# Fetching gates and head outputs earlier in the output projection of a mixture-of-experts attention kernel

## The chip, the cores and the metric

The kernel runs on one core of one Trainium2 chip. The metric is the time of one execution on the device in microseconds (us). All times of the profile come from one profiled execution. Five engines are spoken of: TensorE (PE, with weight loads as PEld), VectorE (DVE), ScalarE (ACT), GpSimd (POOL) and SyncE (SP). SP does nothing here but issue DMAs, one after the other, and wait before an issue when the data or the buffer is not ready.

## The reference

N = 1250 rows of 1024 numbers pass through a graph layer, and then through one transformer layer whose attention has 16 heads of 64, with 8 experts for each head's values and outputs, of which a gate picks two per row. Cut to what matters here:

```
gv, go = gate(x, Wsel_v), gate(x, Wsel_o)          # per row, head, expert: 0 but for the two picked
v   = einsum('bsd,bhse,hedp->bhsp', x, gv, Wv)     # values: gated sum over 8 experts
att = softmax(q k^T / 8)
o   = einsum('bhst,bhtp->bhsp', att, v)
src2 = einsum('bhsp,bhse,hepd->bsd', o, go, Wo)    # outputs: gated sum over heads and experts
```

A residual, a norm, a feed-forward layer with its norm, and a last residual follow. Everything is float32; the kernel splits each operand of a matmul into a high and a low part and adds three products (`dot`, L154 to L156).

## The kernel before, in words

The program is in stages: the graph layer, the gates with the queries and keys, then a long stretch in which values, attention and outputs are interleaved by hand, and the feed-forward layer. The long stretch and most of the outputs lie in `manual_schedule`, where each engine takes its instructions in the order in which the code issues them. Three generators are woven together; each `yield` hands over to the next one.

- `values` makes a head's values in 40 pieces, four for each of ten row tiles (the tenth has 98 rows, the others 128). After a tile's last piece DVE multiplies the product by the gates into `ve` (L897); after every second tile it adds the eight experts in halves, 4, 2 and 1 (L903, L906), and splits the sum into two parts (L908, L909). For the pair with the 98-row tile it does this twice, once for each tile. The weights of the next head are loaded to `w_raw`, rounded on ACT (`w_hi`, L138) and subtracted on DVE (`w_lo`, L144); the fourth block is done in the first pieces of the next head.
- `attention` takes 80 chunks of 256 queries, five for each head, in eight steps each: scores on PE (L721), the maximum on DVE (`most`, L724), the exponential on ACT (`p`, L725), sixteen copies `turned<-p` (L736, eight issued by SP and eight by POOL), a transposition on DVE (L798), a split of the result on ACT and DVE (`att_hi`, L755; `att_lo`, L760), and the products with the values (`po`, L778, evacuated at L785). A chunk's work spreads over the steps of the chunks that follow it.
- `outputs` starts with a preamble of 16 steps beside the last 16 pieces of `values`, and then takes 80 steps m: 16 blocks (eight pairs of heads, four experts at a time) times five chunks of 250 rows. A step multiplies two row tiles, each in two halves; each half is 24 matmuls and one add into the accumulator (L1006), and each step of the main loop holds eight yields.

The pieces of `values` end with head 15; the attention chunks that are left (75 to 79, and two more rounds for what trails) then alternate with the steps of `outputs`, about one step for each chunk. These are the steps from about 1860 to 2010 us.

In `outputs`, `load` issues on SP the gates of a chunk (`gb`, two DMAs of 250 KB, two buffers), the heads' outputs (`oc`, two of 125 KB, one buffer) and the inverse sums (`r`, two of 62.5 KB, one buffer). `gated` (L946 to L948) adds, scales and multiplies them on DVE, in place in `gb`; `parts_of` splits it on ACT and DVE (`go_hi`, L955; `go_lo`, L957). `acc_load` brings a row tile of the running sum (`z_d`, 500 KB by two DMAs at L150). Accumulators 1 to 8 lie in the memory of `zT`, which the last pieces of `values` still read, so the profile names them `zT` and the last one `gate_v`. In step m the order was:

```
            if following:
                found = load(*order[following[0]], following[1])
...
                    nc.vector.tensor_tensor(acc[t][:, cols], acc[t][:, cols], p, ALU.add)
                    if following and half:
                        parts[i] = parts_of(found, i)
                    elif following and i == 0:
                        found = gated(*found)
                    elif raw is not None:
                        after.append(rounded(raw))
```

so that gates, `oc` and `r` of chunk m+1 were all issued at the start of step m, and used by `gated` after the first of the step's four halves. `w_raw` has two buffers.

Of the kernel before, what the change touches and what calls it, by code (L numbers as in the profile page):

```python
# [11 lines left out]
F32 = mybir.dt.float32  # L12
# [5 lines left out]
ALU = mybir.AluOpType  # L18
# [8 lines left out]
HD = 64  # L27
NX = 8
# [4 lines left out]
P = 128  # L33
NT = 10
# [10 lines left out]
QB = 250  # L45
# [27 lines left out]
def gnn_ffn_kernel(  # L73
# [23 lines left out]
    nc = tc.nc  # L97
# [591 lines left out]
    v_of = {}  # L689
# [164 lines left out]
    def values(att_pool, pool, now):  # L854

        todo = {}

        def later(k, what, *args):
            todo.setdefault(k, []).append((what, args))

        piece = 0
        for h in range(H):
            raw, new = {}, [None] * 4

            def load(h, k, raw=raw):
                raw[k] = loaded(wv[h, k])

            def first_part(k, raw=raw, new=new):
                new[k] = high(raw[k])

            def second_part(k, raw=raw, new=new):
                new[k] = rounded(raw.pop(k), None, new[k])

            if h + 1 < H:

                for at_, k in ((22, 0), (36, 1), (37, 2), (39, 3)):
                    later(piece + at_, first_part, k)
                for at_, k in ((23, 0), (37, 1), (38, 2), (40, 3)):
                    later(piece + at_, second_part, k)
                for at_, k in ((16, 0), (22, 1), (28, 2), (37, 3)):  # L880
                    later(piece + at_, load, h + 1, k)
            v_of[h] = att_pool.tile([P, NT, P], F32R, name="v2", bufs=2)

            ts = range(NT) if h < H - 1 else [*range(NZ, NT), *range(NZ)]
            for t in ts:
                n = min(P, N - P * t)
                p = bank([n, 512])
                for d in range(ND):
                    dot(p, z_of(t, d), [part_[:, 512 * (d % 2) : 512 * (d % 2 + 1)] for part_ in now[d // 2]],
                        d == 0, d == ND - 1)  # L890
                    if d % 2 == 0:
                        continue
                    if d == ND - 1:
                        gate = gate_v[:n, t, NX * h : NX * (h + 1)]
                        if t % 2 == 0:
                            ve = pool.tile([P, 2, NX, HD], F32, name="ve", bufs=1)
                        nc.vector.tensor_tensor(ve[:n, t % 2], p.rearrange("p (e k) -> p e k", e=NX),  # L897
                                                gate[:, :, None].to_broadcast([n, NX, HD]), ALU.mult)
                    if d == ND - 1 and t % 2:
                        for n, k in ((P, slice(0, 2)),) if n == P else ((P, slice(0, 1)), (n, slice(1, 2))):  # L900
                            x = ve[:n, k]
                            for half in (4, 2):
                                nc.vector.tensor_tensor(x[:, :, :half], x[:, :, :half], x[:, :, half : 2 * half],  # L903
                                                        ALU.add)
                            v = pool.tile([P, 2, HD], F32, name="v")[:n, k]
                            nc.vector.tensor_tensor(v, x[:, :, 0], x[:, :, 1], ALU.add)  # L906
                            v2 = v_of[h][:n, t - 1 + k.start : t - 1 + k.stop, :]
                            nc.vector.tensor_copy(v2[:, :, :HD], v)  # L908
                            nc.vector.tensor_tensor(v2[:, :, HD:], v, v2[:, :, :HD].bitcast(F32), ALU.subtract)  # L909
                    yield  # L910
                    for what, args in todo.pop(piece, ()):
                        what(*args)
                    piece += 1
            now = new
# [4 lines left out]
    def outputs(acc_pool, pool):  # L919

        last = QW * (NC - 1)

        def load(j, half_e, c):

            cols = slice(QB * c, QB * (c + 1))
            gb = pool.tile([P, 4, QB], F32, name="gb", bufs=2)
            for h2 in range(2):
                row = NX * (2 * j + h2) + 4 * half_e
                g = g_d[row : row + 4, cols]
                nc.sync.dma_start(gb[HD * h2 : HD * (h2 + 1)],  # L930
                                  bass.AP(tensor=g.tensor, offset=g.offset, ap=[[0, HD], [N, 4], [1, QB]]))
            o = pool.tile([P, 2, QB], F32, name="oc")
            for h2 in range(2):
                nc.sync.dma_start(o[HD * h2 : HD * (h2 + 1)], o_d[j][h2][:, cols].rearrange("(m f) n -> f m n", m=2))
            r = pool.tile([P, QB], F32, name="r")
            for h2 in range(2):
                for a, b in ((QB * c, min(QB * (c + 1), last)), (max(QB * c, last), QB * (c + 1))):
                    if b > a:
                        at_ = a + (NC * QW - N if a >= last else 0)
                        nc.sync.dma_start(r[HD * h2 : HD * (h2 + 1), a - QB * c : b - QB * c],  # L940
                                          r_d[j][h2 : h2 + 1, at_ : at_ + b - a].to_broadcast([HD, b - a]))
            return gb, o, r

        def gated(gb, o, r):

            nc.vector.tensor_tensor(o[:, 0], o[:, 0], o[:, 1], ALU.add)  # L946
            nc.vector.tensor_tensor(o[:, 0], o[:, 0], r, ALU.mult)
            nc.vector.tensor_tensor(gb, gb, o[:, 0:1].to_broadcast([P, 4, QB]), ALU.mult)  # L948
            return gb

        def parts_of(gb, i):

            mine = slice(KT * i, KT * (i + 1))
            hi = pool.tile([P, 4, KT], F32R, name="go_hi", bufs=2)
            nc.scalar.copy(hi, gb[:, :, mine])  # L955
            lo = pool.tile([P, 4, KT], F32R, name="go_lo", bufs=2)
            nc.vector.tensor_tensor(lo, gb[:, :, mine], hi.bitcast(F32), ALU.subtract)  # L957
            return hi, lo

        order = [(j, half_e) for j in range(NP) for half_e in range(2)]  # L960
        blocks = {k: [wo[j, 4 * half_e + i] for i in range(4)] for k, (j, half_e) in enumerate(order)}
        steps = [(k, c) for k in range(len(order)) for c in range(NQ)]

        def acc_load(t):
            acc.append(acc_pool(t))
            move(acc[t], z_d[t])


        w, raw = [], []
        for i in range(4):  # L970
            raw.append(loaded(blocks[0][i]))
            yield
            if i % 2:
                yield
                for _ in range(2):
                    w.append(rounded(raw.pop(0)))
                    yield
        found = load(*order[0], 0)
        acc_load(0)
        yield  # L980
        yield
        found = gated(*found)
        yield
        parts = []
        for i in range(2):
            parts.append(parts_of(found, i))
            yield
        after = []
        yield
        for m, (k, c) in enumerate(steps):  # L990
            raw = loaded(blocks[k + 1][c]) if c < 4 and k + 1 < len(order) else None
            following = steps[m + 1] if m + 1 < len(steps) else None
            if following:
                found = load(*order[following[0]], following[1])
            for i in range(2):
                t = 2 * c + i
                if k == 0 and t + 1 < NT:
                    acc_load(t + 1)
                for half in range(2):
                    cols = slice(512 * half, 512 * half + 512)  # L1000
                    p = bank([KT, 512])
                    for e in range(4):
                        dot(p, [part[:, e, :] for part in parts[i]], [part[:, cols] for part in w[e]], e == 0, e == 3)
                        if e == 1:
                            yield
                    nc.vector.tensor_tensor(acc[t][:, cols], acc[t][:, cols], p, ALU.add)  # L1006
                    if following and half:
                        parts[i] = parts_of(found, i)
                    elif following and i == 0:
                        found = gated(*found)  # L1010
                    elif raw is not None:
                        after.append(rounded(raw))
                    yield
            if c == NQ - 1:
                w, after = after, []
# [180 lines left out]
```

## Time and profile before

| what | value |
|---|---|
| median of 3 runs | 3000.13 us (2994.33 to 3004.78) |
| the profiled execution | 2998.75 us |
| its span | 2997.0 us |
| PE busy | 2858.0 us, 95% |
| PEld, DVE | 2357.3 us (79%), 2131.5 us (71%) |
| ACT, POOL | 993.4 us (33%), 568.9 us (19%) |
| granted TensorE clock, mean | 0.981 |
| DMA, mean | 129 GB/s |

The page cuts the span into 40 slices of 75 us; a digit is the busy share in tenths, and PEclk the clock granted to TensorE, also in tenths. In rows of instructions "L946" is line 946 of the kernel, "x2" a count; what stands in brackets is how long the engine stood idle before the row, and what ended that wait. Rows of the windows give the stretch, its length, the busy time of PE, PEld, DVE, ACT and POOL with the number of instructions, the granted clock, the DMA engines' busy share and GB/s.

### The profile page before, as it was taken

The numbers are of one execution on the slowest core, as the hardware profiler recorded it, in microseconds if no ns is written. First come the engines' busy times: TensorE is split into PE (matmuls) and PEld (weight loads), VectorE is DVE, ScalarE is ACT, GpSimd is POOL, SyncE is SP. The second block draws the span as 40 slices with busy tenths as digits, with TensorE's granted clock in tenths as the row PEclk, the third lists the DMA queues.
The fourth block names the chain that finished last, engine by engine and source line by source line (L and its number), as shares of the span: only waits on it lengthen the run. The fifth ranks groups of instructions, "written<-read, shape, count | busy, mean of one in ns | idle before, by whom it ended". The sixth has DMA issues, their size and how long they took to land. (4 is left out here: it accounts for less than half of the span.)

```text
span 2997.0 us, 40469 instructions
## 1 busy us (share of the span) xinstructions
PE 2858.0 (95%) x14018; PEld 2357.3 (79%) x14018; DVE 2131.5 (71%) x3668; ACT 993.4 (33%) x1706; POOL 568.9 (19%) x945
## 2 busy tenths in 40 slices
PE   6989899999999999999999999689999999999998
PEld 5767699978888887888888887567777777777787
DVE  7974488657877877887888778556666666666885
ACT  5772223324434433443434334221111111111222
POOL 2000011113333333333333333210000000000113
PEclk9999899999999999999999999889999999999999
DMA  3115465635555555555555455666444444444412
GB/s 116 56 43 155 145 174 161 194 83 147 139 137 143 136 135 126 136 135 149 138 141 150 129 145 132 156 166 162 114 120 122 116 118 123 113 119 122 108 47 91
DMA packets 229321, 385.46 MB, mean 129 GB/s; under 512 B 43369, under 2 KB 176489, under 8 KB 228946
## 3 DMA queue, kind: packets, MB, share of 16 engines
q1 hardware_dynamic: 176898, 273.49, 32.9%
q0 software_dynamic: 51888, 104.18, 14.5%
q10 hardware_dynamic: 320, 5.12, 0.5%
q8 instruction: 111, 1.82, 0.3%
q14 instruction: 104, 0.85, 0.1%
HBM read 220.73 MB, written 62.16 MB: 94 GB/s over the span
## 5 line engine op out<-in xcount | busy, mean ns | idle before, releaser
L155 PE MATMUL mm<-w_lo,zT 128*128 128x512 f32 (+1 forms) x1280 | 507.1, 396 | 13.1 <-DVE w_lo L144 13.1
L154 PE MATMUL mm<-w_hi,go_hi 128*125 128x512 f32 x1280 | 508.2, 397 | 2.1 <-ACT go_hi L955 1.2
L155 PE MATMUL mm<-w_lo,go_hi 128*125 128x512 f32 x1280 | 509.0, 398 | 0.0
L154 PE MATMUL mm<-w_hi,zT 128*128 128x512 f32 (+1 forms) x1280 | 507.4, 396 | 1.0 <-ACT w_hi L138 1.0
L156 PE MATMUL mm<-w_hi,go_lo 128*125 128x512 f32 x1280 | 506.6, 397 | 0.7 <-DVE go_lo L957 0.7
L156 PE MATMUL mm<-w_hi,zT 128*128 128x512 f32 (+1 forms) x1280 | 506.0, 395 | 0.0
L755 ACT CAST att_hi<-turned 128x512 fp32r<-128x512 f32 x400 | 239.5, 621 | 439.7 <-DVE turned L798 257.3
L736 POOL DMA_DIRECT2D turned<-p x640 | 342.5, 543 | 79.7 <-ACT p L725 44.3
L1006 DVE TENSOR_TENSOR zT<-zT,mm 125x512 f32<-125x512 f32 x256 | 175.1, 685 | 221.5 <-PE mm L156 217.5
L955 ACT CAST go_hi<-gb 128x500 fp32r<-128x500 f32 x160 | 98.3, 615 | 669.0 <-PE mm L155 280.5
L725 ACT ACTIVATE p<-side,most 128x1250 f32<-128x1250 f32 x160 | 209.0, 1306 | 330.4 <-DVE most L724 325.8
L724 DVE TENSOR_REDUCE most<-side 128x1 f32<-128x1250 f32 x160 | 230.9, 1443 | 113.1 <-PE side L721 111.9
L798 DVE STREAM_TRANSPOSE turned<-turned 128x1280 f32<-128x1280 f32 x160 | 232.4, 1490 | 111.0 <-DMA q<-kq_d 52.7
L154 PEld LDWEIGHTS mm<-w_hi,go_hi 128*125 128x125 f32 x1280 | 239.2, 187 | 63.2 <-ACT go_hi L955 1.5
L156 PEld LDWEIGHTS mm<-w_hi,go_lo 128*125 128x125 f32 x1280 | 238.8, 187 | 62.1 <-DVE go_lo L957 1.1
L155 PEld LDWEIGHTS mm<-w_lo,go_hi 128*125 128x125 f32 x1280 | 239.0, 187 | 59.3
L156 PEld LDWEIGHTS mm<-w_hi,zT 128*128 128x128 f32 (+1 forms) x1280 | 238.4, 186 | 59.7
L155 PEld LDWEIGHTS mm<-w_lo,zT 128*128 128x128 f32 (+1 forms) x1280 | 238.8, 187 | 53.2 <-DVE w_lo L144 18.2
L154 PEld LDWEIGHTS mm<-w_hi,zT 128*128 128x128 f32 (+1 forms) x1280 | 238.8, 187 | 36.0 <-ACT w_hi L138 1.2
L760 DVE TENSOR_TENSOR att_lo<-turned,att_hi 128x512 fp32r<-128x512 f32 x400 | 262.1, 681 | 0.0
L721 PE MATMUL side<-keys,q 128*128 128x512 f32 (+1 forms) x960 | 215.3, 360 | 30.5 <-ACT p L725 30.5
L721 PEld LDWEIGHTS side<-keys,q 128*128 128x128 f32 x960 | 182.9, 191 | 74.4 <-ACT p L725 32.7
(234 smaller groups left out, 4640.2 us busy)
## 6 DMA issues: line engine op xcount, KB each, us to landing
turned<-p SPq DMA_DIRECT2D x640, 80.0 KB
turned<-p POOLq DMA_DIRECT2D x640, 80.0 KB, 3.3
gb<-g_d SPq DMA_DIRECT2D x160, 250.0 KB
w_raw<-in_wv SPq DMA_DIRECT2D x64, 512.0 KB
w_raw<-in_wo SPq DMA_DIRECT2D x64, 512.0 KB
q<-kq_d POOLq DMA_DIRECT2D x80, 256.0 KB, 4.3
oc<-o_d SPq DMA_DIRECT2D x160, 125.0 KB
kq_d<-qk_hi SPq DMA_DIRECT2D x64, 156.2 KB
```

The lines of the kernel that those rows point to most:

```text
L154: nc.tensor.matmul(p, lhsT=lhs[0], rhs=rhs[0], start=start, stop=False)
L155: nc.tensor.matmul(p, lhsT=lhs[0], rhs=rhs[1], start=False, stop=False)
L156: nc.tensor.matmul(p, lhsT=lhs[1], rhs=rhs[0], start=False, stop=stop)
L721: nc.tensor.matmul(side[:, k0 : k0 + w], lhsT=q_of[n][:, part, P * i : P * (i + 1)], rhs=keys[:, k0 : k0 + w], start=(part == 0), stop=(pa ...
L724: nc.vector.tensor_reduce(most, side[:, :N], AX.X, ALU.max, negate=True)
L725: nc.scalar.activation(p[:, (2 * n + i) % 3, :N], side[:, :N], AF.Exp, bias=most, accum_out=inverse[h][:, 2 * c + i : 2 * c + i + 1])
L736: queue.dma_start(t[NB * a : NB * (a + 1), :, KA * b : KA * (b + 1)], both[NB * b : NB * (b + 1), :, KA * a : KA * (a + 1)])
L755: nc.scalar.copy(hi, x)
L760: nc.vector.tensor_tensor(lo, x, hi.bitcast(F32), ALU.subtract)
L798: nc.vector.transpose(turned[n][:, i], turned[n][:, i])
L955: nc.scalar.copy(hi, gb[:, :, mine])
L1006: nc.vector.tensor_tensor(acc[t][:, cols], acc[t][:, cols], p, ALU.add)
```

## The change

There are four edits.

1. `load` becomes `load_gates` and `load_o`, and step m fetches for chunk m+2. Its gates are issued at the start of step m; its `oc` and `r` right behind `gated` of chunk m+1.
2. Accumulators are loaded two row tiles ahead instead of one: 0 and 1 in the preamble, t+2 in the first five steps.
3. The preamble keeps its 16 steps and is written out by number. The first two weight blocks are rounded in the same steps as before (numbers 3 and 4); blocks 2 and 3 are loaded in those steps (before: 5 and 6), and rounded in 7 and 8 (before: 8 and 9). Chunk 0 is fetched in step 4, accumulator 0 in 5 (both before: 10), `gated` runs in 9 (before: 12), and chunk 1 is fetched there. Step 6 is the one in which the attention issues eight of its `turned` copies on SP.
4. In `values` one `ve` tile is made once, and the adds over the experts run over all 128 rows of both tiles of a pair, also for the pair with the 98-row tile. Rows 98 to 127 of that tile hold what an earlier tile left; the products read only the first 98.

```diff
-                        for n, k in ((P, slice(0, 2)),) if n == P else ((P, slice(0, 1)), (n, slice(1, 2))):
-                            x = ve[:n, k]
-                            for half in (4, 2):
-                                nc.vector.tensor_tensor(x[:, :, :half], x[:, :, :half], x[:, :, half : 2 * half],
-                                                        ALU.add)
...
+                        for half in (4, 2):
+                            nc.vector.tensor_tensor(ve[:, :, :half], ve[:, :, :half], ve[:, :, half : 2 * half],
+                                                    ALU.add)
+                        v = pool.tile([P, 2, HD], F32, name="v")
+                        nc.vector.tensor_tensor(v, ve[:, :, 0], ve[:, :, 1], ALU.add)
+                        v2 = v_of[h][:, t - 1 : t + 1, :]
...
+        def fetch(m, gates):
+            if m < len(steps):
+                (j, half_e), c = order[steps[m][0]], steps[m][1]
+                if gates:
+                    found.append(load_gates(j, half_e, c))
+                else:
+                    held[:] = load_o(j, c)
+
+        w, raw, found, held, parts = [], [], [], [], []
+        for begun in range(16):
+            if begun < 2:
+                raw.append(loaded(blocks[0][begun]))
+            if begun in (3, 4, 7, 8):
+                w.append(rounded(raw.pop(0)))
+            if begun in (3, 4):
+                raw.append(loaded(blocks[0][begun - 1]))
+            if begun == 4:
+                fetch(0, True)
+                fetch(0, False)
+            if begun == 5:
+                acc_load(0)
+            if begun == 9:
+                current = gated(found.pop(0), *held)
+                fetch(1, True)
+                fetch(1, False)
+            if begun in (11, 13):
+                parts.append(parts_of(current, len(parts)))
+            if begun == 14:
+                acc_load(1)
             yield
         after = []
-        yield
         for m, (k, c) in enumerate(steps):
             raw = loaded(blocks[k + 1][c]) if c < 4 and k + 1 < len(order) else None
-            following = steps[m + 1] if m + 1 < len(steps) else None
-            if following:
-                found = load(*order[following[0]], following[1])
+            following = m + 1 < len(steps)
+            fetch(m + 2, True)
             for i in range(2):
                 t = 2 * c + i
-                if k == 0 and t + 1 < NT:
-                    acc_load(t + 1)
+                if k == 0 and t + 2 < NT:
+                    acc_load(t + 2)
...
                     if following and half:
-                        parts[i] = parts_of(found, i)
+                        parts[i] = parts_of(current, i)
                     elif following and i == 0:
-                        found = gated(*found)
+                        current = gated(found.pop(0), *held)
+                        fetch(m + 2, False)
```

More of the change, by code (lines that the diff above doesn't have):

```diff
@@ L861, in values @@
         piece = 0
+        ve = pool.tile([P, 2, NX, HD], F32, name="ve", bufs=1)
         for h in range(H):
@@ L894, in values @@
                         gate = gate_v[:n, t, NX * h : NX * (h + 1)]
-                        if t % 2 == 0:
-                            ve = pool.tile([P, 2, NX, HD], F32, name="ve", bufs=1)
                         nc.vector.tensor_tensor(ve[:n, t % 2], p.rearrange("p (e k) -> p e k", e=NX),
@@ L899, in values @@
                     if d == ND - 1 and t % 2:
-                        for n, k in ((P, slice(0, 2)),) if n == P else ((P, slice(0, 1)), (n, slice(1, 2))):
-                            x = ve[:n, k]
-                            for half in (4, 2):
-                                nc.vector.tensor_tensor(x[:, :, :half], x[:, :, :half], x[:, :, half : 2 * half],
-                                                        ALU.add)
[L905 to L909, printed above, removed]
+                        for half in (4, 2):
[4 more added lines that the diff above has]
+                        v2 = v_of[h][:, t - 1 : t + 1, :]
+                        nc.vector.tensor_copy(v2[:, :, :HD], v)
+                        nc.vector.tensor_tensor(v2[:, :, HD:], v, v2[:, :, :HD].bitcast(F32), ALU.subtract)
                     yield
@@ L921, in outputs, with load_gates @@
         last = QW * (NC - 1)
-        def load(j, half_e, c):
+        def load_gates(j, half_e, c):
             cols = slice(QB * c, QB * (c + 1))
@@ L931, in load, with load_o @@
                                   bass.AP(tensor=g.tensor, offset=g.offset, ap=[[0, HD], [N, 4], [1, QB]]))
+            return gb
+        def load_o(j, c):
+            cols = slice(QB * c, QB * (c + 1))
             o = pool.tile([P, 2, QB], F32, name="oc")
@@ L941, in load @@
                                           r_d[j][h2 : h2 + 1, at_ : at_ + b - a].to_broadcast([HD, b - a]))
-            return gb, o, r
+            return o, r
         def gated(gb, o, r):
@@ L966, in acc_load @@
             move(acc[t], z_d[t])
-        w, raw = [], []
-        for i in range(4):
-            raw.append(loaded(blocks[0][i]))
-            yield
[L973 to L981, printed above, removed]
-        found = gated(*found)
[L983 to L986, printed above, removed]
+        def fetch(m, gates):
[26 more added lines that the diff above has]
+                acc_load(1)
             yield
         after = []
-        yield
         for m, (k, c) in enumerate(steps):
             raw = loaded(blocks[k + 1][c]) if c < 4 and k + 1 < len(order) else None
-            following = steps[m + 1] if m + 1 < len(steps) else None
-            if following:
-                found = load(*order[following[0]], following[1])
+            following = m + 1 < len(steps)
+            fetch(m + 2, True)
             for i in range(2):
                 t = 2 * c + i
-                if k == 0 and t + 1 < NT:
-                    acc_load(t + 1)
+                if k == 0 and t + 2 < NT:
+                    acc_load(t + 2)
                 for half in range(2):
@@ L1007, in outputs @@
                     if following and half:
-                        parts[i] = parts_of(found, i)
+                        parts[i] = parts_of(current, i)
                     elif following and i == 0:
-                        found = gated(*found)
+                        current = gated(found.pop(0), *held)
+                        fetch(m + 2, False)
                     elif raw is not None:
```

## The prediction

> **What bounds the kernel now.** I read the page first: how busy TensorE (PE) is, where it is not, and at what clock.
>
> ```profile
> PE 2858.0 (95%) x14018; PEld 2357.3 (79%) x14018; DVE 2131.5 (71%) x3668; ACT 993.4 (33%) x1706; POOL 568.9 (19%) x945
> ...
> PE   6989899999999999999999999689999999999998
> ...
> PEclk9999899999999999999999999889999999999999
> ```
>
> PE is the bound nearly everywhere; an edit beside a full PE is worth nothing. Slices 26 to 28 (from about 1870 us) are the hole in the stretch that the change touches: the "6" and "8", with a lowered clock. There the last attention chunks run beside the first output steps. Next, the stage windows, a steady attention chunk (15 us) against one turn-to-turn cycle of the hole:
>
> ```profile
> 1825.00:1840.00 15.00, 15.00 (x77) 12.67 (x77) 11.71 (x16) 5.95 (x10) 5.62 (x11) 1.00 0.48 109
> ...
> 1922.19:1949.93 27.74, 17.63 (x77) 14.42 (x76) 15.45 (x20) 7.81 (x14) 5.58 (x10) 0.76 0.60 150
> ```
>
> Both hold about 77 matmuls, yet the second takes 27.74 us. PE is busy for 17.63 of it (stretched by a granted clock of 0.76), VectorE (DVE) for 15.45, and the DMA engines for 0.60 x 27.74 = 16.6. No resource fills the cycle, so a chain of waits does. The waits of 1840 to 2060 us:
>
> ```profile
> ACT p L725 <- DVE most L724: 63.0, 11, 15.8
> ...
> DVE oc L946 <- DMA oc<-o_d: 38.8, 5, 10.3
> ...
> PE side L721 <- ACT p L725: 30.3, 4, 10.1
> ```
>
> PE waits for the exponentials, these for the row maximum on DVE, and DVE stands in `gated` before a load. Its timeline:
>
> ```profile
> 1901.18 0.69 DVE L1006 TENSOR_TENSOR acc<-acc,mm 125x512 f32<-125x512 f32 x1
> 1910.93 0.42 DVE L946 TENSOR_TENSOR oc<-oc 128x250 f32<-128x250 f32 x1 [9.06 <-DMA oc<-o_d]
> 1911.77 0.42 DVE L947 TENSOR_TENSOR oc<-oc,r 128x250 f32<-128x250 f32 x1 [0.43 <-DMA r<-r_d]
> ...
> 1913.34 1.45 DVE L724 TENSOR_REDUCE most<-side 128x1 f32<-128x1250 f32 x1
> ```
>
> And the sync queue (SP) shows why the load is late: it is issued behind eight transposing copies, a weight block and 500 KB of gates, right before its use.
>
> ```profile
> 1894.77 5.17 SPq L736 DMA_DIRECT2D turned<-p  x8
> 1899.99 0.60 SPq L127 DMA_DIRECT2D w_raw<-in_wo  x1
> 1900.63 1.87 SPq L930 DMA_DIRECT2D gb<-g_d  x2
> 1902.60 1.43 SPq L934 DMA_DIRECT2D oc<-o_d  x2
> 1904.08 1.25 SPq L940 DMA_DIRECT2D r<-r_d  x2
> 1905.43 4.39 SPq L150 DMA_DIRECT2D zT<-z_d  x4
> ```
>
> From issue (1902.60) to the end of the wait is 8.3 us. After about 2040 us the windows show PE at 60.00 of every 60 us until 2820, so nothing in those steps can win time.
>
> **Part 1, fetches ahead.** Today step m issues gates, `oc` and `r` for chunk m+1 at its start; `gated` uses them a quarter of a step later. After the change gates have a step and a quarter, and `oc` and `r`, issued behind `gated` of m+1, have a full step, 11.2 us even at PE's pace (48 matmuls by 0.233 from start to start) and more beside attention. With 8.3 us from issue to landing in the worst burst shown, the DVE wait goes. Only the order changes: per step the same 7 or 8 DMAs on SP, and none more on POOL.
>
> Its size, on the adds behind each step's first half (L1006): 1901.18, 1927.63, 1956.72, 1984.06, 2005.29, thus 26.5, 29.1, 27.3 and 21.2, together 104.1 us. In the cycles from one L946 to the next, 27.7, 27.5 and 26.2 us, the waits for `oc` and `r` are 10.8, 9.0 and 7.8; 16.9, 18.4 and 18.3 us remain. What comes next is no longer one wait: DVE needs 15.5 us busy, PE about 15.9 (48 x 0.233 for outputs, 12 score and 20 product matmuls at about 0.235 or 0.118 from start to start, 4.7), the DMA engines 16.6, SP's issues 14.7 (the six lines above). I take 18 us for each full cycle, which leaves DVE 2.5 us of its small waits (0.60 for `w_hi`, up to 1.9 for a matmul, both in the old cycles), and 15 for the last one, which has no new softmax. So 104.1 - (3 x 18 + 15) = **35 us**. Best case: cycles of 16.6 and 13.7, 40 us. Worst credible: 21 and 17, 24 us.
>
> The waits that this adds: gates of m+2 wait on SP for the buffer of chunk m, last read by `go_lo` at the end of step m-1; `oc`/`r` wait for `gated` on DVE, as each has one buffer. Behind them on SP stand the second accumulator load, the next weight block and the next eight `turned` copies, which in turn wait for the second softmax, later in DVE's order than `gated`: nothing that could start is held up. The price if it could: at most the interval from the start of a step to its first add, about 3 us per cycle, 12 in all. The accumulators a step earlier (1 MB per step either way) are hidden the same way: their first use is a step later; uncovered, each would cost its 2.2 us of issue, some 10 us in all.
>
> Two rules of the Trainium skill bear on this size. The granted clock fell to 0.76 in the cycle above and single matmuls went from 0.39 to 0.63 us. "TensorE: Matmul & The Clock Gate" (Part 1: The HAM clock gate) says that PE falls to half clock after about 3.4 us without work. With PE's gaps (8.8, 10.1, 8.4, 4.6 us) gone the clock returns, worth 17.63 - 15.9 = 1.7 us per cycle on PE; I add none, because DVE, not PE, sets 18, and it already covers it. Against the change stands "DMA: Bandwidth & Descriptors" (Issuing engines are not separate DMA queues): all queues end on the same 16 DMA engines, so a new order moves no byte faster. By its fabric ceiling of 435 GB/s the 4.17 MB of a cycle would take 9.6 us and never bind; by the trace they take 16.6. I use 16.6: a cycle cannot be much under it. That is why I stay above DVE's and PE's own sums, and why rival 1 is not small.
>
> **Part 2, first weights' loads.** Today load 3 stands on SP behind the `turned` copies (issued at 1875.38); ScalarE waits 5.63 us for it, DVE 6.32, and PE stands 3.0 us at 1885.36 and 4.0 at 1895.57. In the new order load 3 goes out when its buffer is free (`w_lo` of block 1, done at about 1868), and lands in some 4.1 us (load 0: 1858.99 to 1863.05), before it is wanted. Moved ahead of the same eight `turned` copies: load 3 (0.5 us of issue), two gates (1.3), two `oc` (1.4), two `r` (1.6), two accumulator copies (1.4), 6.2 us from 1867.5, so the copies start at about 1873.8, not 1870.17, and land near 1881. DVE's transposition of them, at 1887.06 today, comes due at about 1881 once its 6.3 us wait is gone. Net **6 us** (0 if the copies land 6 us later still; at most 10.8: those two PE gaps and 3.8 of slowed matmuls). The 3.1 us PE gap at 1870 stays: load 0 is where it was. Accumulator 1 is now asked for one piece before the last reader of its memory; SP holds for about 2 us, with the next weight block behind it, which is wanted ten us later: nothing.
>
> **Part 3, sums over all rows.** For the last pair of row tiles ten DVE instructions become five. Rows cost nothing: 98x512 and 128x512 both take 681 ns at L897. The ten take 904.23 to 907.15, 2.92 us; the five, as in other pairs (1897.90 to 1899.88), 1.98. So DVE is 0.94 us earlier once per head, right before each head switch:
>
> ```profile
> 904.23 0.74 DVE L903 TENSOR_TENSOR ve<-ve 128x256 f32<-128x256 f32 x2
> ...
> 907.15 0.69 DVE L760 TENSOR_TENSOR att_lo<-turned,att_hi 128x512 fp32r<-128x512 f32 x1
> 907.76 1.22 DVE L144 TENSOR_TENSOR w_lo<-w_raw,w_hi 128x1024 fp32r<-128x1024 f32 x1
> ...
> 909.03 0.50 PE L155 MATMUL mm<-w_lo,zT 128*128 128x512 f32 x1 [0.85 <-DVE w_lo L144]
> ```
>
> PE waits for exactly this `w_lo` at 14 switches, 0.73 to 0.85 us each. `w_lo` also needs `w_hi` from ScalarE (ready at 906.33 here, so it can start at 906.82). Switch by switch, the earlier of the two limits gives the whole wait in ten, 0.35 to 0.7 in three and nothing in one (at 1644.90), 9.7 us in all. I take **9**, between 3 (if ScalarE's load is late more often) and 9.7.
>
> **Sum.** 35 + 6 + 9, and 1 for two PE gaps of 0.9 and 0.7 us at 2019 and 2040 behind the same loads: 51 us. The profiled execution took 2998.75 us (span 2997.0), 1.4 under the median of 3000.13; so 2948 for such an execution, 2949 as a median. The end of the program is left as it is, give or take 3 us.
>
> **Rivals.** (1) The DMA engines bind: 16.6 us of work in an 18 us cycle, in bursts. For: single 10 us windows at a share of 1.06, and DVE's small waits for `turned` copies even in steady chunks. Against: the bursts now get the idle parts of the cycle. Cycles of 21, 24 us saved, 3 in part 2, 8 in part 3: 2965.
> (2) It doesn't do what it says: the wait for `oc` moves to `turned` or to the accumulators, cycles stay at 27, only part 3 remains: 2991. Against: the DMA engines are idle for 40% of each cycle.
> (3) Slower: in the 75 steps after 2040 us, today PE-bound, `oc`'s single buffer lets its load start only after `gated`. Of 11.2 us some 3 go to `gated` and issuing, 8 remain. If landing takes x us more than that, each step loses x; slower than before by over 0.3% from x = (51 + 9) / 75 = 0.8 us; at x = 1.1, 3031. For: 8.3 us were seen. Against: that was in a burst at a share near 1; in those steps the share is 0.44.
>
> **How the numbers follow.** Main case 0.58 (2936 to 2958), rival 1 0.24 (2957 to 2982), rival 2 0.07, rival 3 0.11. 0.3%, 9 us, is about what a measurement of this kernel can tell from no change. Faster 0.83 (main, rival 1 and a little of 2), same 0.06, slower 0.11. The range 2935 to 2984 leaves out rivals 2 and 3 and a thin tail. Its low end is the sum of best cases: 40 + 10.8 + 9.7 + 1.6 + 3 = 65.
>
> **What would show it.** Right: L946's wait for `oc` gone, cycles at 17 to 19 us, clock near 1.0 from 1890 on, PE's waits for `w_lo` L144 down from 13.1 us to about 4. Wrong: `turned` (L798) waiting for DMA several us per cycle (rival 1), or L946 waiting after 2040 us with PE under 60 of 60 (rival 3).

## The result, and the profile after

The median went from 2998.39 us (4 runs) to 2963.11 us (4 runs; 2959.1 to 2975.35), ratio 0.9887 with a 95% interval of 0.9853 to 0.9922. A second set, on another occasion, gave 2960.35 against 3000.68 us, 0.9875 (0.9858 to 0.9893). The profiled execution took 2961.16 us, span 2959.4, against 2998.75 and 2997.0 before.

So 38 us of the 51 forecast came by the profiled executions (35 by these medians, 40 by those of the second set). To see where, I cut both traces at the same instructions: the exponential (L725) of the first chunk, that of chunk 75, the add behind step 0's first half, that of step 4, and the end.

| stretch (us) | before | after | saved | forecast |
|---|---|---|---|---|
| start to first exponential | 633.7 | 633.7 | 0.0 | 0 |
| chunks 0 to 74 beside `values` (the head stage) | 1224.1 | 1222.3 | 1.8 | 9 (part 3) |
| chunk 75 to the add of step 0 (preamble) | 43.3 | 41.0 | 2.3 | 6 (part 2) |
| adds of steps 0 to 4 | 104.1 | 69.3 | 34.8 | 35 (part 1) |
| from there to the end | 991.7 | 993.0 | -1.3 | 1 |

From the page of the changed kernel, the slices of TensorE (PE) and its clock:

```profile
PE   6989899999999999999999999899999999999998
...
PEclk9999899999999999999999999999999999999999
```

The hole is nearly filled (slices 26 and 27 went from 6 and 8 to 8 and 9), and with the gaps the clock loss went. One cycle of it in the windows (stretch, length, busy time of PE, PEld, DVE, ACT, POOL with counts, clock, DMA share, GB/s), from one L949 to the next (the old L946):

```profile
1914.44:1931.86 17.42, 16.15 (x82) 13.20 (x81) 15.46 (x21) 7.82 (x13) 5.63 (x11) 1.00 0.97 223
```

27.7 us have become 17.42, with PE busy for 16.15, DVE for 15.46 and the DMA engines at a share of 0.97. All three are nearly full, so little is left to win in this cycle by order alone. On DVE `gated` now follows the add without a wait:

```profile
1913.84 0.69 DVE L1018 TENSOR_TENSOR zT<-zT,mm 125x512 f32<-125x512 f32 x1 [0.72 <-PE mm L156]
1914.44 0.41 DVE L949 TENSOR_TENSOR oc<-oc 128x250 f32<-128x250 f32 x1
1914.89 0.42 DVE L950 TENSOR_TENSOR oc<-oc,r 128x250 f32<-128x250 f32 x1
1915.35 1.20 DVE L951 TENSOR_TENSOR gb<-gb,oc 128x1000 f32<-128x1000 f32 x1
```

because SP issued its data a cycle ago. In SP's rows below, `oc` and `r` (from 1919.55) are for the `gated` at 1931.86:

```profile
1908.91 6.19 SPq L736 DMA_DIRECT2D turned<-p  x8
1915.14 1.27 SPq L127 DMA_DIRECT2D w_raw<-in_wo  x1
1916.52 1.33 SPq L928 DMA_DIRECT2D gb<-g_d  x2
1917.89 1.56 SPq L150 DMA_DIRECT2D zT<-z_d  x2
1919.55 1.25 SPq L937 DMA_DIRECT2D oc<-o_d  x2
1920.84 3.71 SPq L943 DMA_DIRECT2D r<-r_d  x2
```

Part 3 is the one that failed. PE's waits between 640 and 1850 us, in the head stage (who waited for whom, us in total, times, longest), before:

```profile
PE mm L155 <- DVE w_lo L144: 13.1, 16, 1.2
PE po L778 <- ACT o L785: 12.1, 17, 3.3
```

and after:

```profile
PE po L778 <- ACT o L785: 19.2, 21, 3.7
PE mm L155 <- DVE w_lo L144: 3.9, 7, 0.8
```

The wait for `w_lo` fell by 9.2 us, as worked out; the wait for `o` rose by 7.1. At a head switch of the changed kernel one sees where the freed DVE time goes. The sums end earlier, `w_lo` starts at 907.03 (907.76 before), the maximum at 908.77 (909.49 before):

```profile
904.41 1.15 DVE L901 TENSOR_TENSOR ve<-ve 128x512 f32<-128x512 f32 x2
...
907.03 1.22 DVE L144 TENSOR_TENSOR w_lo<-w_raw,w_hi 128x1024 fp32r<-128x1024 f32 x1
...
908.77 1.45 DVE L724 TENSOR_REDUCE most<-side 128x1 f32<-128x1250 f32 x1
...
913.89 1.51 DVE L798 STREAM_TRANSPOSE turned<-turned 128x1280 f32<-128x1280 f32 x1 [2.47 <-DMA q<-kq_d]
```

and then DVE stands for 2.47 us before the transposition, where the kernel before stood for 0.72:

```profile
912.86 1.51 DVE L798 STREAM_TRANSPOSE turned<-turned 128x1280 f32<-128x1280 f32 x1 [0.72 <-DMA q<-kq_d]
```

Of the 1.75 us more, 0.72 are the freed time; the transposition also came 1.03 us later at this switch, where SP took 7.31 us to issue its eight copies, 5.86 before (why is not shown). The row names the DMA that was last by the profile; what the transposition needs are the sixteen copies of L736. That suggested a loop, from chunk to chunk: second exponential, sixteen copies, transposition, next maximum, next exponential. Worked out from the rows of chunks 1 to 71 as medians, in the kernel before: exponential 1.3 us; from its end 10.14 us to the start of the transposition (SP has issued its eight copies after 5.9, POOL after 6.3, the last packets of both are done after 8.8 and 8.6, POOL's copies are reported landed after 9.1); two transpositions to 2.8 us later; the maximum right behind them, 0 us later, 1.4; then the next exponential. Sum 15.7. In means it is 16.4, because in one chunk of each head SP's copies are out only 8.0 us after the exponential and the transposition comes after 12.2; a chunk takes 1224.1 / 75 = 16.3 us. PE's own work is about 15.85 (PE was busy for 15.83 per chunk in half_copies below, where it hardly waits). With such a loop DVE time off the loop is worth nothing. In the changed kernel the mean from the exponential to the transposition is the same as before (10.61 and 10.62 us), and DVE's mean wait before the transposition rose from 1.46 to 1.69 us per chunk: five chunks of 0.23 are about the time that the sums free per head.

### The profile page after: what moved, and what is told of

The parts are those of the page before. It is cut to its first block, busy times and chain, and to the rows that moved or that the text cites. A ratio compares the mean times of both kernels' runs of the same rounds, so it can differ in the third digit from the quotient of the medians.

```text
span 2959.4 us, 40398 instructions
## 1 busy us (share of the span) xinstructions
PE 2849.7 (96%) x14018; PEld 2349.2 (79%) x14018; DVE 2120.9 (72%) x3588; ACT 993.0 (34%) x1706; POOL 569.1 (19%) x945
## 5 line engine op out<-in xcount | busy, mean ns | idle before, releaser
L736 POOL DMA_DIRECT2D turned<-p x640 | 342.5, 542 | 80.8 <-ACT p L725 44.3
L798 DVE STREAM_TRANSPOSE turned<-turned 128x1280 f32<-128x1280 f32 x160 | 232.4, 1490 | 135.7 <-DMA q<-kq_d 57.5
L725 ACT ACTIVATE p<-side,most 128x1250 f32<-128x1250 f32 x160 | 209.2, 1307 | 289.4 <-DVE most L724 284.7
L778 PE MATMUL po<-att_hi,v 128*128 128x256 f32 (+1 forms) x800 | 215.0, 290 | 33.8 <-ACT o L785 33.5
L144 DVE TENSOR_TENSOR w_lo<-w_raw,w_hi 128x1024 fp32r<-128x1024 f32 x154 | 189.5, 1231 | 43.6 <-ACT w_hi L138 43.3
```

Of the source, the lines that this page charges most:

```text
L144: (lo_engine or nc.vector).tensor_tensor(lo, raw, hi.bitcast(F32), ALU.subtract)
L725: nc.scalar.activation(p[:, (2 * n + i) % 3, :N], side[:, :N], AF.Exp, bias=most, accum_out=inverse[h][:, 2 * c + i : 2 * c + i + 1])
L736: queue.dma_start(t[NB * a : NB * (a + 1), :, KA * b : KA * (b + 1)], both[NB * b : NB * (b + 1), :, KA * a : KA * (a + 1)])
L778: nc.tensor.matmul(po, lhsT=v_of[h][:rows, t, :], rhs=part[:rows, :, NB * b : NB * (b + 1)], start=(first and b == 0 and part is parts[0]) ...
L798: nc.vector.transpose(turned[n][:, i], turned[n][:, i])
```

## The experiments

Theory: the head stage is held by the loop through the copies, and the preamble by what DMA has to move in it; only the cycles of steps 0 to 4 were held by the order of SP's queue. Rival: PE and DVE hold the head stage, as the prediction had it, and the 9 us were lost by chance elsewhere. Ratios are to the kernel before, run on the same chip.

**Part 3 alone (sums_only).** The kernel before with this edit:

```diff
-                        for n, k in ((P, slice(0, 2)),) if n == P else ((P, slice(0, 1)), (n, slice(1, 2))):
-                            x = ve[:n, k]
...
+                        for half in (4, 2):
+                            nc.vector.tensor_tensor(ve[:, :, :half], ve[:, :, :half], ve[:, :, half : 2 * half], ALU.add)
```

> The kernel before with only the sums over all rows (DVE done 0.94 us earlier once per head). Loop theory: from chunk to chunk the head stage is held by a loop (exponential, transposing copies, DVE transposition, row maximum, next exponential), so the freed DVE time is waited away before the transposition and the PE gap at the head switch reappears before the product that waits for the evacuation of po: 0 to -3 us, PE's waits for w_lo near 4.7 us, those for o above 19 us. PE theory (as predicted): -8 to -10 us.

3001.11 against 3001.31 us, ratio 0.9997 (0.9988 to 1.0006; 14 and 20 runs). The interval, -3.6 to +1.8 us, holds the loop theory and excludes 9 us. PE's waits in the head stage:

```profile
PE po L778 <- ACT o L785: 18.1, 25, 2.2
PE mm L155 <- DVE w_lo L144: 2.9, 4, 0.9
```

Together 21.0 us, 25.2 before: the wait mostly changed its name (and PE's busy time in the stage rose by 2.6 us).

**Parts 1 and 2 alone (fetch_only).** The changed kernel with that edit taken back.

```diff
-                        for half in (4, 2):
-                            nc.vector.tensor_tensor(ve[:, :, :half], ve[:, :, :half], ve[:, :, half : 2 * half], ALU.add)
...
+                        for n, k in ((P, slice(0, 2)),) if n == P else ((P, slice(0, 1)), (n, slice(1, 2))):
+                            x = ve[:n, k]
```

> The changed kernel with the old sums (twice for the last pair): only the fetches and the preamble. Loop theory: within 3 us of the changed kernel, so 33 to 38 us under the kernel before. PE theory: 9 us slower than the changed kernel, so about 27 us under the kernel before.

2969.68 us, ratio 0.9893 (0.9874 to 0.9912), 31.6 us under the kernel before by the medians. Both expectations lie near; the interval, 26 to 38 us, doesn't separate them. In its trace the head stage took 1227.7 us, 5.4 more than in the changed kernel; but eight traces that all have the new sums, and the same program up to chunk 75, gave 1220.9 to 1231.4 there, so one trace can't size a few us. Sums_only decides this point.

**The store of o behind the copies (store_late).** An attempt to shorten the loop:

```diff
...
-            if before:
-                product(n - 2, 4)
+            store = product(n - 2, 4) if before else None
             if now:
                 turn(n)
...
+            if store:
+                store()
...
```

> The changed kernel with one more edit: on POOL the store of a chunk's o is issued behind the eight transposing copies of the next chunk instead of ahead of them, so that they start about 1.5 us earlier. Loop theory: the transposition on DVE starts 1 to 1.5 us earlier after the exponential (10.2 us now), DVE's wait before it falls under 0.7 us, the chunk period falls from 16.2 towards PE's 15.85, and the time falls by 10 to 25 us. PE theory: the copies are not what holds the stage, no change within 4 us.

2986.51 us, 0.9948 (0.9928 to 0.9968): slower than the changed kernel by 18 to 26 us (by the ratios and by the medians). The expectation of a gain was wrong, and that is what made this run useful. POOL's copies were indeed out by 4.7 us after the exponential, not 6.3, but SP's eight took until 7.05, not 5.99, and the last packet of SP's copies moved from 8.8 to 9.7. The later half counts: the transposition started after 10.85 us (10.18), DVE's mean wait rose to 2.09, and the head stage took 1245.6 us, 23 more, or 0.31 per chunk. PE's waits for `o` in the stage grew from 19.2 to 35.1 us. The edit changes only the order of POOL's issues, and ACT never waits in the stage for the later store to free `o`. So it is the landing of the copies that sets the time of the stage: the loop is there.

**The same with the old sums (store_late_old_sums).**

```diff
@@ store_late, values @@
...
+                        for n, k in ((P, slice(0, 2)),) if n == P else ((P, slice(0, 1)), (n, slice(1, 2))):
...
```

> As the store_late kernel, with the old sums. Loop theory: with the loop shortened DVE's order in front of the head switch counts again, so this is 5 to 9 us slower than store_late. If the sums are worth nothing there either: within 3 us of store_late.

2989.28 us, 0.995 (0.9932 to 0.9967), not separable from store_late. Since the loop had become longer, not shorter, its premise didn't hold; that the sums are worth little beside a longer loop fits the theory, and no more follows.

**Part 2 taken back (old_preamble), with the changed kernel again (changed_again) as base.**

```diff
@@ changed_again: no edit; old_preamble, in the preamble: @@
-            if begun in (3, 4, 7, 8):
+            if begun in (3, 4, 8, 9):
                 w.append(rounded(raw.pop(0)))
...
-            if begun == 4:
+            if begun == 10:
                 fetch(0, True)
                 fetch(0, False)
+                acc_load(0)
...
```

> The changed kernel once more, as the base of the other kernels of this set: 2961 to 2966 us.

> The changed kernel with the preamble in the old order (blocks 2 and 3 loaded in steps 5 and 6 and rounded in 8 and 9, chunk 0 and accumulator 0 fetched in 10, gated in 12), chunk 1 fetched behind gated, accumulator 1 after the last step. It undoes part 2 alone. If part 2 is worth what the two traces show (2.3 us): 2 to 4 us slower than the changed kernel. If it is worth the 6 us predicted: 6 us slower or more. The old gaps of PE at the scores and at the product (3.0 and 4.0 us) should come back and the 5.6 us gap go.

2960.35 us, 0.9875 (0.9858 to 0.9893), and 2967.60 us, 0.9890 (0.9875 to 0.9905). In the traces the preamble takes 41.7 and 42.6 us and the adds of steps 0 to 4 take 69.4 and 72.4: part 2 is worth 1 to 2 us in its own stretch and perhaps 4 with the cycles behind it. The 7 us between the medians hold more than that; 8.8 us of the two traces' difference lie in chunks 0 to 74, where the two programs are the same. The traced execution of old_preamble was also the slowest of its four, and the intervals of the two ratios overlap. So part 2's worth is only bounded, at about 1 to 7 us. PE's gap of 5.6 us before the product went, as expected; but in place of the old 3.0 and 4.0 there is one of 6.1 us before the scores and one of 0.8.

**Fetches behind the copies (fetch_behind_copies).**

```diff
-            if begun == 4:
+            if begun == 6:
                 fetch(0, True)
                 fetch(0, False)
-            if begun == 5:
+            if begun == 10:
                 acc_load(0)
```

> The changed kernel with chunk 0 fetched in preamble step 6 (on SP behind the eight transposing copies of that step, not ahead of them) and accumulator 0 in step 10. Theory: part 2 lost most of its gain because 1.4 MB of fetches stand ahead of the copies, which DVE awaits (4.6 us before the transposition, 5.6 us of PE); with the copies first the DVE wait falls to about 1 us and PE's gap at the product from 5.6 to 2 us or less: 3 to 5 us faster than the changed kernel. Rival: the copies land late in any case (SP holds them until the fourth weight block's buffer is free), no change within 1 us in the trace.

2969.71 us, 0.9896 (0.9881 to 0.9912), 9 us slower than its base. The preamble took 44.6 us (41.7). In the changed kernel the two roundings follow each other, as foreseen, and then the copies are late:

```profile
1871.37 2.36 DVE L144 TENSOR_TENSOR w_lo<-w_raw,w_hi 128x1024 fp32r<-128x1024 f32 x2
...
1883.51 2.90 DVE L798 STREAM_TRANSPOSE turned<-turned 128x1280 f32<-128x1280 f32 x2 [4.59 <-DMA gb<-g_d]
```

With the copies first, `oc` is:

```profile
1883.03 0.42 DVE L949 TENSOR_TENSOR oc<-oc 128x250 f32<-128x250 f32 x1 [9.35 <-DMA oc<-o_d]
```

PE's gap of 5.6 us before the product is gone, and one of 10.6 us before the scores stands in its place. What comes second is waited for. Neither theory as I wrote it held (the gain didn't come, and the copies weren't the only thing that was late).

**The rounding later (preamble_spread).**

```diff
-            if begun in (3, 4, 7, 8):
+            if begun in (5, 7, 8, 12):
                 w.append(rounded(raw.pop(0)))
-            if begun in (3, 4):
-                raw.append(loaded(blocks[0][begun - 1]))
-            if begun == 4:
+            if begun in (5, 7):
+                raw.append(loaded(blocks[0][len(raw) + len(w)]))
+            if begun == 6:
                 fetch(0, True)
                 fetch(0, False)
...
```

> The changed kernel with the preamble's rounding later: blocks 0 to 3 rounded in steps 5, 7, 8, 12, blocks 2 and 3 loaded in 5 and 7, chunk 0 fetched in 6, gated in 9, accumulator 0 in 10. Theory: also PE's first gap (3.2 us, the product waits for o, whose copy on ScalarE stands behind the rounding of block 0, which waits 3.8 us for its load) goes: 6 to 9 us faster than the changed kernel. Rival: DVE's own work fills the preamble (33 us of it in 16 steps), so less than 3 us.

2970.98 us, 0.9909 (0.9893 to 0.9925), slower again; preamble 45.9 us. PE's gap of 3.2 us for `o` was gone, and one of 10.9 us for the scores stood later. Three orders of the preamble, three places for the wait.

**Gates not ahead (gates_one_ahead).**

```diff
-            fetch(m + 2, True)
+            fetch(m + 1, True)
...
-                fetch(1, True)
                 fetch(1, False)
```

> The changed kernel with gates fetched at the start of step m for chunk m+1 (as before), and oc and r still right behind the chunk just multiplied. If both loads have to be early: gated waits for gates instead, 5 to 7 us per cycle (they are issued 2.6 us before oc was, and are 500 KB), 20 to 28 us slower than the changed kernel. If only oc and r were late (last in their queue): within 5 us of the changed kernel.

2988.63 us, 0.9958 (0.9944 to 0.9973): 28 us slower than the changed kernel of the other set, and the adds of steps 0 to 4 took 97.1 us, 28 more. Waits between 1840 and 2030 us:

```profile
DVE gb L951 <- DMA gb<-g_d: 31.9, 4, 9.4
```

Both halves of part 1 were needed. With `oc` early alone the wait goes over to the gates, 8 us a cycle.

**Half of the copies' bytes left out (half_copies).** Half of the attention's exponentials never reach the products.

```diff
...
-            both = p[:, first : second + 1 : second - first, :]
+            own = (2 * n + 1) % 3
+            both = p[:, own : own + 1, :]
...
-                    queue.dma_start(t[NB * a : NB * (a + 1), :, KA * b : KA * (b + 1)],
+                    queue.dma_start(t[NB * a : NB * (a + 1), 1:, KA * b : KA * (b + 1)],
```

> The changed kernel with half of the transposing copies' bytes left out: each of the sixteen moves the second block of a chunk's exponentials alone (40 KB, not 80), the other half of the buffer stays as it was set once; the attention's result is left wrong for it. Same instructions on all engines. Loop theory: the copies are what sets the head stage's pace, so DVE's transposition starts earlier after the exponential (10.2 us now, under 9), its wait before it shrinks from 1.7 us, and the stage falls towards PE's 15.85 us per chunk: 10 to 26 us faster than the changed kernel up to chunk 75. PE theory: only the cycles after chunk 75 gain, a few us.

2928.44 us, 0.9760 (0.9745 to 0.9775). The head stage took 1195.7 us, 27 less, 15.94 per chunk; DVE had no wait before the transposition, and PE's waits in the stage were:

```profile
PE mm L155 <- DVE w_lo L144: 6.2, 15, 0.8
PE po L781 <- ACT o L788: 1.1, 1, 1.1
```

With the copies lighter the wait for `o` is gone and PE sets the pace. The preamble fell to 33.6 us too (41.0), which the theory had not been asked for: there also the copies' bytes were in the way. The adds of steps 0 to 4 took 63.8 us.

**The store late at the end only (store_late_at_end).**

```diff
...
+            if store and n < 75:
+                store()
             if now:
                 turn(n)
...
+            if store and n >= 75:
+                store()
...
```

> The changed kernel with the store of o behind the copies (as in store_late), from chunk 75 on alone. In store_late the head stage lost 22 us but the steps from the exponential of chunk 75 to the add of step 4 took 106.0 us, against 110.3 and 111.1 in the changed kernel. If both parts stand on their own: 4 to 5 us faster than the changed kernel. If that gain was a result of the slower stage ahead: no change.

2963.91 us, 0.9879 (0.9864 to 0.9894). The stretch from chunk 75 to step 4 took 108.1 us, against 110.3 and 111.1 in the changed kernel, not 106. No gain that the medians show.

**The copies in two halves (copies_in_halves).** What half_copies points to, with nothing left out: the first exponential's half goes out as soon as it is there.

```diff
...
+            if n < EARLY:
+                turn(n, 0)
             yield
...
             if now:
-                turn(n)
+                turn(n, 1 if n < EARLY else 2)
```

> The changed kernel with every chunk's transposing copies (up to chunk 74) in two sets of sixteen: those of the first exponential right behind it, those of the second behind the second, so that the same bytes move but only half of them stand between the second exponential and DVE's transposition. Twice the DMA issues: some 10.5 us of SP's 16 us per chunk, 9 us of POOL's. Loop theory: as in half_copies the last copy lands under 8 us after the exponential, DVE's wait for it goes, the stage runs at PE's pace: 15 to 26 us faster than the changed kernel, faster than both kernels. Rival: the queues' own issue time or the first set's traffic delays the second set, and the stage is no faster or slower (up to +20).

2933.79 us, 0.9786 (0.9770 to 0.9801): 64 us under the kernel before and 27 to 29 under the changed kernel. All bytes move, in twice as many DMAs, and the head stage still takes only 1194.6 us. PE's and DVE's waits in it:

```profile
PE mm L155 <- DVE w_lo L144: 6.7, 15, 0.8
PE po L783 <- ACT o L790: 1.1, 1, 1.1
```

```profile
DVE turned L803 <- DMA turned<-p: 2.7, 3, 1.5
```

In the changed kernel the waits before the transposition (L798) are put down to four DMAs:

```profile
DVE turned L798 <- DMA q<-kq_d: 55.3, 31, 5.9
DVE turned L798 <- DMA turned<-p: 43.9, 24, 3.8
DVE turned L798 <- DMA r_d<-rows: 14.3, 11, 2.2
...
DVE turned L798 <- DMA w_raw<-in_wv: 7.1, 3, 2.6
```

These four rows sum to 120.6 us; with the halves 3.8 are left (the 2.7 of the row shown, and 0.6 and 0.5 put down to `w_raw` and `r_d`). What mattered in half_copies was not how many bytes move in a chunk, but how many stand between the second exponential and the transposition.

## Why the prediction was right, and where it was not

The measured 2963 us lies in the stated range, but outside the main case's own 2936 to 2958 and inside the band of rival 1, whose mechanism did not happen. The largest part was right in cause and size. That the whole fell within the range is owed to part 1 and to the width of the range; the reasons given for parts 2 and 3 did not hold.

- **Bound and cause in the hole: right.** The wait of DVE for `oc` in the cycles of steps 0 to 4 is gone and both early fetches were needed for it (gates_one_ahead).
- **Part 1, 35 us: right, 34.8.** Cycles of 16.8, 17.4, 17.8 and 17.3 us against 18, 18, 18 and 15. The last one was longer than taken: DVE waited 3.0 us for `turned` copies in it. The clock came back (1.00 in the cycle shown); what it added by itself was not separated. The DMA engines, at a share of 0.97, are the third full resource, for which 16.6 us had been set.
- **Part 2, 6 us: mis-sized.** Its own stretch gained 2.3 us in the first trace. The step that failed is "they land near 1881". The late fourth weight block is no longer waited for, but the transposition came at 1883.51, in a program that was 1.3 us ahead by its first weight load and 1.8 by its exponential, so about 4 us later than taken. I had timed the copies by SP's issue alone. POOL's half, issued up to 9.8 us after the exponential, was reported landed only after 14.2, against 9.1 in a usual chunk, with the DMA engines at a share of 1.06 from 1870 to 1880. My bound of zero was for this case. The sign stood in the trace of before: there POOL's half was reported landed at 1886.39, 16.3 us after its exponential, and DVE, done by 1885.08 with what it had to do behind the late weight block, waited for it 1.98 us more:

```profile
1887.06 2.90 DVE L798 STREAM_TRANSPOSE turned<-turned 128x1280 f32<-128x1280 f32 x2 [1.98 <-DMA r<-r_d]
```

  Ending the wait of 6.3 us could not move this transposition; only earlier copies could.
- **Part 3, 9 us: the step failed.** "DVE is 0.94 us earlier" was nearly right (`w_lo` started 0.73 us earlier at the switch shown), "PE waits for exactly this `w_lo`" was right, and `w_lo`'s wait fell as worked out. Wrong was the tacit step from there: that PE, once a gap is closed, stays ahead. The page's 95% for PE had been read as "PE is the bound nearly everywhere". The head stage was held by a loop through the copies, with PE 0.45 us per chunk short of it, and the loop hands the gap to the next place. The sign was in the trace of before: DVE stood about 1.4 us before the transposition in a typical chunk, and the maximum followed it without a gap. Shown by sums_only (no gain), store_late (later copies, slower stage), half_copies and copies_in_halves (earlier copies, PE's pace).
- **The small gaps at 2019 and 2040 us: wrong by 1 us.** Both are still there, 0.87 and 0.74 us; one `oc` is still waited for 3.6 us. SP's rows put the feed-forward's constants among these fetches; that they are the reason was not tried.
- **The rivals.** Rival 1's 2965 is near the time, but its mechanism is not what happened: the cycles took 17.3 us on average, not 21. The DMA's hold was in the head stage and the preamble. Rival 2 didn't happen. Rival 3 didn't: from step 5 to the last add the two kernels take the same time within 1 us.
- Not run: the old sums on top of copies_in_halves. There PE sets the pace, so the 9 us might then appear; that is open.

## What to carry to other kernels

A queue that issues a load right before its use can be cured by order alone, but then every load in the same use must go ahead. When one engine is 95% busy and the rest is many short gaps, add up the loop that leads from one round to the next, through DMA too, before counting a closed gap as a gain: if the loop is as long as the round, the gap moves. To shorten such a loop, send what is ready early ahead of time, so that less stands between the last producer and the first consumer.

## What the runs showed of the hardware that was not expected

- Copies issued by one engine can slow the issuing of another, not just its data: with POOL's eight copies started about 1.5 us earlier (store_late), SP took 0.81 us for each of its eight in place of 0.68, was done 7.05 us after the exponential in place of 5.99, and its last packet moved from 8.8 to 9.7. The stage paid 0.31 us per chunk.
- Twice as many DMAs of half the size (32 of 40 KB per chunk in place of 16 of 80 KB) cost the head stage nothing that shows: 1194.6 us, against 1195.7 with sixteen of 40 KB.
